# Layer 2 of a four-layer graph network: each node's own weights are formed and multiplied in four column tiles, after all supports

## The chip, the cores and the metric

The kernel runs on one core of one Trainium2 chip. The core has a matrix engine (TensorE, PE in the profile; its weight loads are listed apart as PEld), three elementwise engines (VectorE = DVE, ScalarE = ACT, GpSimd = POOL), a queue engine (SyncE = SP) and DMA queues. PE writes only to PSUM, a small memory of eight banks of 512 floats per partition; DVE and ACT carry results from PSUM to SBUF, the large on-chip memory. The metric is the device time of one execution in microseconds; lower is better. Before the change it is 1935.28 us, the median of 3 runs (1935.16 to 1940.87).

## The reference, cut to what matters

The input `x` is 8 x 2048 x 64 (batch B, nodes N, features), `adj` is a 2048 x 2048 matrix of zeros and ones. Four layers follow one another, each as `x = layernorm(x + layer(x, adj))`. The change is in layer 2 (a Chebyshev graph convolution with weights of its own for every node) and at the beginning of layer 3:

```python
def _L2_gnn_ref(x, node_embeddings, lap, weights_pool, bias_pool):   # lap = adj, CHEB_K = 3
    support_set = [jnp.eye(N, dtype=x.dtype), lap]
    for _ in range(2, CHEB_K):
        support_set.append(2.0 * lap @ support_set[-1] - support_set[-2])
    apt = jax.nn.softmax(jax.nn.relu(node_embeddings @ node_embeddings.T), axis=1)
    support_set.append(apt)
    supports = jnp.stack(support_set, axis=0)
    weights = jnp.einsum('nd,dkio->nkio', node_embeddings, weights_pool)
    bias = node_embeddings @ bias_pool
    x_g = jnp.einsum('knm,bmc->bknc', supports, x)
    x_g = jnp.transpose(x_g, (0, 2, 1, 3))
    out = jnp.einsum('bnki,nkio->bno', x_g, weights) + bias
    return out
```

`node_embeddings` is 2048 x 16 (d), `weights_pool` is 16 x 4 x 64 x 64 (d, k, i, o). So a node's output is a row of 4 x 64 = 256 support values times a 256 x 64 matrix, and that matrix is the sum of 16 pool matrices weighted by the node's embedding. Layer 3 takes three steps of `v = relu([v, adj v] W1 + b1) W2 + b2`.

## The kernel before, in words

**Data.** The batches go in pairs p = 0..3, so that 2 x 64 features fill the 128 partitions or the 128 columns of a tile. `adj` stays in SBUF for the whole kernel as 16 row tiles of 128 x 2048 in a form in which PE multiplies at one pass ("F32R"); the operand beside it is split into a high and a low part (`x_part[c]`, tags `v0h` to `v3l`), and both parts are multiplied. Nodes go in four chunks c of 512 columns, each with four tiles j of 128. A product with `adj` for one pair is 128 matmuls of 512 columns.

**PE order.** Every matmul and transpose goes through the helpers `mm` (L171) and `transpose` (L174), which pin PE to the order in which the program is written; `pin` does the same for a few operations of other engines. `later(n, f)` runs f after n further matmuls of the kind that call `tick`. PSUM has two pools here: `lps` with four one-bank buffers (tag `mm`) and `pph` with two two-bank buffers (tag `ph`).

**Layer 2.** The support `apt` is multiplied first (`ua`, plain float32). Then the function `supports()` is a generator: for each pair it yields the products `adj x` and `adj (adj x)`, one matmul at a time, and stores x, `adj x`, `adj adj x` and `apt x`, turned so that features are on partitions, into `xt_hbm`, `u1_hbm`, `u2_hbm`, `u3_hbm`. `fill(n)` takes n matmuls from it. The main loop of layer 2 (p, c, b, j, k) multiplies a tile of 128 nodes of one batch by the whole pool: the 256 support values are contracted in two matmuls (q = 0, 1), `wp[q][k]` holds 32 outputs x 16 embedding entries = 512 columns, and `py` receives, for each node and output, the 16 partial values. DVE then multiplies `py` by the node's 16 embedding entries (L1350) and adds the 16 up (L1351). After each such pair of matmuls `fill(2)` lets two matmuls of the supports through, as long as there are any.

```python
for q in range(2):
    mm(py, lhsT=a_z[q][:, cols(j, P)], rhs=wp[q][k], start=q == 0, stop=q == 1)
tick()
pr = fcav.rearrange("p i b f -> p (i b f)").rearrange("p (o d) -> p o d", d=D)
nc.vector.tensor_tensor(pr, py, e_b, ALU.mult)
nc.vector.tensor_reduce(r[:, j, b, cols(k, OH)], pr, AX.X, ALU.add)
fill(2)
```

At the end of a chunk the layer norm is taken (DVE L1362, ACT L148, DVE L150, POOL's power L154, DVE L155) and written back to `xn[p]`. The pool is centred beforehand (L1281 to L1289), so that the mean of the outputs is zero.

**Layer 3.** For p = 0, `first(c, n)` turns chunk c of `xn[0]` (`first_h`) and multiplies it by part of W1 (`factor`, which writes `x_part[c]`). The step loop accumulates `u` over all 16 tiles of `adj`, applies relu (L1506, L1508) and goes on. Between its tiles, `check()` compares a piece of `adj` with its rounded form.

Of the kernel before, what the change touches and what calls it, by code (L numbers as in the profile page):

```python
# [56 lines left out]
def tile_gnn_fast(  # L57
# [13 lines left out]
    w_pool: bass.AP,  # L71
# [152 lines left out]
    for i in range(12):  # L224
# [13 lines left out]
    xt_hbm, u1_hbm, u2_hbm, u3_hbm = (  # L238
        [dram.tile([P, N], F32, name=f"{name}_hbm{p}") for p in range(NP)] for name in ("xt", "u1", "u2", "u3")
    )  # L240
# [8 lines left out]
    adj = [adj_tile(adj_pool, t) for t in range(NT - XT)]  # L249
# [806 lines left out]
    xn += [xnp.tile([P, NT, P], F32, name=f"xn{p}") for p in range(NP)]  # L1056
# [141 lines left out]
    ready = set()  # L1198

# [7 lines left out]
    def turned_x(p, c):  # L1207
        pt = lps.tile([P, C], F32, tag="mm", name="pt", bufs=4)
        for j in range(JT):
            transpose(pt[:, cols(j, P)], xn[p][:, c * JT + j, :])  # L1210
        out_t(xt_hbm[p], c, pt, nc.scalar)

        bias = l2.tile([P, JT, 1, F], F32, tag="bias", name="bias", bufs=1)
        nc.sync.dma_start(bias[:, :, 0, :], bias_hbm[:, wide(c), :])
        x4 = xn[p][:, wide(c), :].rearrange("p t (b f) -> p t b f", f=F)
        nc.gpsimd.tensor_tensor(x4, x4, bias.to_broadcast([P, JT, 2, F]), ALU.add)

    def supports():

        for p in range(NP):  # L1220
            for k, hbm in ((1, u1_hbm), (2, u2_hbm)):
                chunks = [2, 3, 0, 1] if p == 0 and k == 1 else [*range(NCH)]
                uts = {}
                for g in range(2):
                    own = (2 * g, 2 * g + 1)
                    ug = pph.tile([P, 2, C], F32, tag="ph", name="u", bufs=2)
                    for q in chunks:
                        for t in range(q * JT, (q + 1) * JT):
                            for i in range(2):
                                for c in own:  # L1230
# [6 lines left out]
                                    yield  # L1237
                        if k == 1 and g == 0:
# [11 lines left out]
                    ready.add((p, k, g))  # L1250

    filler = supports()

    def until(*what):
        while what not in ready:
            fill(1)
# [7 lines left out]
    OD = F * D  # L1264
    OH = C // D
    emb_n = l2.tile([P, NT, D], F32, tag="e", name="emb_n")
    nc.gpsimd.dma_start(emb_n, emb.rearrange("(t p) d -> p t d", p=P))

# [7 lines left out]
    wp = [[l2.tile([P, OH, D], F32, tag=f"w{2 * q + k}", name=f"wp{q}{k}") for k in range(2)] for q in range(2)]  # L1276
    for q in range(2):
        for k in range(2):
            nc.gpsimd.dma_start(wp[q][k].rearrange("p o d -> p (o d)"), w_pool[q * P:(q + 1) * P, cols(k)])
    for k in range(2):  # L1280
        nc.vector.tensor_tensor(wp[0][k][0:F], wp[0][k][0:F], wp[1][k][0:F], ALU.subtract)  # L1281
        nc.vector.tensor_scalar(wp[1][k][0:F], wp[1][k][0:F], 2.0, None, op0=ALU.mult)
    sums = l2.tile([P, 2, 2, D], F32, tag="m", name="wp_m")
    for q in range(2):
        for k in range(2):
            nc.vector.tensor_reduce(sums[:, q, k, :], wp[q][k].rearrange("p o d -> p d o"), AX.X, ALU.add)
        nc.vector.tensor_tensor(sums[:, q, 0, :], sums[:, q, 0, :], sums[:, q, 1, :], ALU.add)
        for k in range(2):
            nc.vector.scalar_tensor_tensor(  # L1289
                wp[q][k], sums[:, q, 0:1, :].to_broadcast([P, OH, D]), -1.0 / F, wp[q][k],  # L1290
                op0=ALU.mult, op1=ALU.add,
            )

    halves = [slice(b * F, (b + 1) * F) for b in range(2)]
    lower, upper = halves
    xg = {}

    def load_xg(p, c, b):

        until(p, 2, c // 2)  # L1300
        a, z = (l2.tile([P, C], F32, tag=f"g{2 * b + q}", name=f"xg{b}{q}") for q in range(2))
        for dst, src in ((a[lower], xt_hbm), (a[upper], u1_hbm), (z[lower], u2_hbm), (z[upper], u3_hbm)):
            nc.sync.dma_start(dst, src[p][halves[b], cols(c)])
        xg[b] = a, z
# [29 lines left out]
    for b in range(2):  # L1334
        load_xg(0, 0, b)
    fill(20)
    for p in range(NP):
        for c in range(NCH):
            r = staged("r").rearrange("p t (b f) -> p t b f", f=F)
            for b in range(2):  # L1340
                a_z = xg[b]
                for j in range(JT):
                    e_b = emb_n[:, c * JT + j:c * JT + j + 1, :].to_broadcast([P, OH, D])
                    for k in range(2):
                        py = lps.tile([P, OH, D], F32, tag="mm", name="py", bufs=4)
                        for q in range(2):
                            mm(py, lhsT=a_z[q][:, cols(j, P)], rhs=wp[q][k], start=q == 0, stop=q == 1)
                        tick()
                        pr = fcav.rearrange("p i b f -> p (i b f)").rearrange("p (o d) -> p o d", d=D)
                        nc.vector.tensor_tensor(pr, py, e_b, ALU.mult)  # L1350
                        nc.vector.tensor_reduce(r[:, j, b, cols(k, OH)], pr, AX.X, ALU.add)  # L1351
                        fill(2)
                    if p == NP - 1 and c == NCH - 1 and b == 1 and j in (1, 2):

                        first(j - 1, 2)
                if c + 1 < NCH:
                    load_xg(p, c + 1, b)
                elif p + 1 < NP:
                    load_xg(p + 1, 0, b)
            r3 = r.rearrange("p t b f -> p t (b f)")  # L1360
            xs = xn[p][:, wide(c), :]
            nc.vector.tensor_tensor(r3, r3, xs, ALU.add)  # L1362
            layernorm(va, grouped(r3), grouped(xs), centred=True, small=l2, tag="x", bufs=2)

    STEPS = 3
    for c in (2, 3):  # L1370
# [892 lines left out]
```

## Time and profile before

| what | value |
|---|---|
| median of 3 runs | 1935.28 us (1935.16 to 1940.87) |
| span of the profiled execution (first to last instruction) | 1931.4 us |
| mean granted PE clock in it | 0.986 of full speed |
| busy in the span: PE / DVE / POOL / ACT | 1863.2 / 1010.8 / 533.5 / 393.9 us |
| layer 2's `apt` product | about 520 to 745 us |
| supports alone, then supports mixed with the pool product | 760 to 808 us, then 808 to about 1450 us |
| layer 3 | about 1450 us to the end |

The profiled execution has no time of its own beside its span; the median of the unprofiled runs lies 3.9 us above that span.

How to read it: the page gives busy time by engine, the chain of work that ended last, and groups of equal instructions. A row of a group reads: line, engine, operation, output <- inputs, shapes, count, then busy time and the mean duration of one in ns, then the idle time before it. A float32 matmul appears as two records. The duration of a PE record contains its way through the array, which overlaps with that of the next one; what a matmul costs in a stream is the distance from start to start.

### The profile page before, as it was taken

Reading aid. Unit: us, or ns where it says so; the run is one execution under the profiler, and the core shown is the slowest. Engines: PE = TensorE matmul, PEld = TensorE weight load, DVE = VectorE, ACT = ScalarE, POOL = GpSimd, SP = SyncE. Lnnn points to the kernel's source line nnn. Section 1 sums busy time; section 2 is a strip of 40 time slices with the busy share of each in tenths; the row PEclk is TensorE's granted clock in tenths of the full one; section 3 lists DMA queues with packets and bytes.
Section 4 is the critical chain, followed back from the end, with each engine's and each line's share of the span. In section 5 each row is a group of like instructions: output and inputs, shape, how many; then the busy total and the mean of one; then the engine's idle time right before and its main releaser. Section 6 shows DMA issues by size and latency. Waiting matters only on the chain.

```text
span 1931.4 us, 19557 instructions
## 1 busy us (share of the span) xinstructions
PE 1863.2 (96%) x7100; PEld 1211.2 (63%) x7100; DVE 1010.8 (52%) x1741; ACT 393.9 (20%) x771; POOL 533.5 (28%) x480
## 2 busy tenths in 40 slices
PE   6889899998999999999999999999999999999996
PEld 4667666666644445755755565565447878887875
DVE  6788756777422221466367636645784343333432
ACT  1446344343211111100100000010002222222211
POOL 3688645665344444111001101100001020100201
PEclk8999999999999999999999999999999999999998
DMA  9833343443300001211111110111101121121211
GB/s 321 292 92 115 124 150 123 158 143 118 98 0 28 28 22 45 93 44 52 45 36 52 56 45 22 60 56 36 44 22 41 44 60 44 50 54 45 57 26 24
DMA packets 94185, 143.10 MB, mean 74 GB/s; under 512 B 29232, under 2 KB 40112, under 8 KB 93696
## 3 DMA queue, kind: packets, MB, share of 16 engines
q1 hardware_dynamic: 83920, 105.39, 17.9%
q0 software_dynamic: 7760, 27.66, 4.4%
q10 hardware_dynamic: 2400, 8.72, 1.3%
q8 instruction: 58, 0.95, 0.2%
q14 instruction: 47, 0.39, 0.1%
HBM read 98.67 MB, written 43.06 MB: 73 GB/s over the span
## 4 chain that ended last, share of the span: by engine, by line
PE 83%; DMA 2%; DVE 1%; issue 1%; POOL 1%; ACT 1%; POOLq 0%; SPq 0%; ACTq 0%; DVEq 0%
PE u L171 37%; PE py L171 23%; PE ua L171 11%; PE ug L171 3%; PE pr L171 2%; PE pf L171 1%; PE po L171 1%; PE pt L174 1%; PE s L171 1%; PE pd L171 1%; PE pi L171 1%; DMA x<-x_hbm 0%; PE pn L174 0%; DMA xn<-in_emb 0%; PE pg L174 0%
## 5 line engine op out<-in xcount | busy, mean ns | idle before, releaser
L171 PE MATMUL py<-wp,xg 128*128 128x512 f32 x1024 | 475.2, 592 | 0.8 <-DMA xg<-u_hbm 0.8
L171 PEld LDWEIGHTS py<-wp,xg 128*128 128x128 f32 x1024 | 193.3, 189 | 161.5 <-issue 138.6
L1350 DVE TENSOR_TENSOR fcav<-py,emb_n 128x512 f32<-128x512 f32 x256 | 176.9, 691 | 135.1 <-PE py L171 129.3
L171 PE MATMUL ua<-pt,xn 128*128 128x512 f32 x512 | 230.2, 592 | 1.5 <-DVE pt L1131 1.5
L1351 DVE TENSOR_REDUCE r<-fcav 128x32 f32<-128x512 f32 x256 | 175.6, 686 | 8.2
L171 PEld LDWEIGHTS ua<-pt,xn 128*128 128x128 f32 x512 | 96.9, 190 | 111.2 <-issue 104.2
L154 POOL TENSOR_TENSOR ln_r<-ln_e,neg_half 128x8 f32<-128x8 f32 x32 | 53.5, 1671 | 399.2 <-DVE ln_e L152 369.8
L171 PE MATMUL u<-adj,v0h 128*128 128x512 f32 x384 | 148.0, 453 | 1.3 <-ACT h L1506 1.3
L171 PE MATMUL u<-adj,v2l 128*128 128x512 f32 x384 | 140.7, 431 | 1.3 <-DVE v2l L167 1.3
L171 PE MATMUL u<-adj,v2h 128*128 128x512 f32 x384 | 141.8, 436 | 0.0
L171 PE MATMUL u<-adj,v3l 128*128 128x512 f32 x384 | 140.1, 429 | 0.0
L171 PE MATMUL u<-adj,v3h 128*128 128x512 f32 x384 | 139.6, 430 | 0.0
L171 PE MATMUL u<-adj,v1h 128*128 128x512 f32 x384 | 139.3, 430 | 0.0
L171 PE MATMUL u<-adj,v0l 128*128 128x512 f32 x384 | 138.9, 429 | 0.0
L171 PE MATMUL u<-adj,v1l 128*128 128x512 f32 x384 | 137.9, 425 | 0.0
L1131 DVE TENSOR_SCALAR pt<-pt 128x512 f32<-128x512 f32 x64 | 30.3, 474 | 150.5 <-ACT pt L1130 150.3
L1137 POOL TENSOR_TENSOR acc<-acc,pt 128x512 f32<-128x512 f32 x60 | 76.4, 1274 | 107.1 <-DVE pt L1131 106.4
L1432 DVE SCALAR_TENSOR_TENSOR ar<-fcav,ar 128x512 f32<-128x512 f32 x64 | 45.7, 714 | 107.3 <-ACT ar L1431 107.3
L171 PEld LDWEIGHTS u<-adj,v0h 128*128 128x128 f32 x384 | 70.8, 189 | 37.4 <-issue 24.9
L171 PEld LDWEIGHTS u<-adj,v2l 128*128 128x128 f32 x384 | 72.9, 191 | 31.2 <-issue 14.9
L171 PEld LDWEIGHTS u<-adj,v3l 128*128 128x128 f32 x384 | 72.6, 190 | 30.2 <-issue 15.7
L171 PEld LDWEIGHTS u<-adj,v3h 128*128 128x128 f32 x384 | 72.8, 190 | 28.9 <-issue 14.3
(360 smaller groups left out, 2724.8 us busy)
## 6 DMA issues: line engine op xcount, KB each, us to landing
adj<-in_adj_t POOLq DMA_DIRECT2D x32, 512.0 KB, 6.9
fcav<-in_adj_t SPq DMA_DIRECT2D x64, 256.0 KB, 2.9
u_hbm<-ut SPq DMA_DIRECT2D x48, 256.0 KB, 2.4
xg<-u_hbm SPq DMA_DIRECT2D x96, 128.0 KB, 2.9
x_hbm<-r SPq DMA_DIRECT2D x28, 256.0 KB, 2.3
hs_hbm<-st ACTq DMA_DIRECT2D x8, 584.0 KB, 4.8
xt<-in_x_t SPq DMA_DIRECT2D x16, 256.0 KB, 6.0
ut<-u_hbm SPq DMA_DIRECT2D x16, 256.0 KB, 3.6
```

Of the source, the lines that this page charges most:

```text
L154: nc.gpsimd.tensor_tensor(rstd, vare, neg_half[:, :groups], ALU.pow)
L171: tc.keep_in_program_order(nc.tensor.matmul(*args, **kw))
L174: tc.keep_in_program_order(nc.tensor.transpose(dst, src, ident))
L1131: nc.vector.tensor_scalar(pt, pt, 1.0, None, op0=ALU.max)
L1137: nc.gpsimd.tensor_tensor(accs[c], accs[c], pt, ALU.add)
L1350: nc.vector.tensor_tensor(pr, py, e_b, ALU.mult)
L1351: nc.vector.tensor_reduce(r[:, j, b, cols(k, OH)], pr, AX.X, ALU.add)
L1432: nc.vector.scalar_tensor_tensor(ar.bitcast(F32), seen_a, 1.0, ar.bitcast(F32), op0=ALU.mult, op1=ALU.not_equal, accum_out=left[:, t, k:k ...
```

## The change

All supports now come first: the generator runs to its end before anything of the weights' product starts. Its gaps on the other engines take in, as a list `aside`, the preparation of the pool and of the embeddings.

Then come 16 units u = (c, k): eight node chunks c of 256 nodes, and two halves k of the contraction (x and `adj x`; `adj adj x` and `apt x`). Each unit has two parts.

- `produce` forms the weights of its 256 nodes: for each output o a matmul of 64 rows (16 embedding entries in four combinations of high and low parts) x 128 columns (two supports x 64 inputs), 256 nodes wide, in F32R. Two of them, for two outputs, lie in the lower and the upper half of PE's rows. ACT and DVE carry the PSUM results into `w_all` (128 partitions x 256 nodes x 64 outputs), three copies in five on ACT. A copy takes 2 outputs x 256 nodes and writes them node by node, 64 floats apart.
- `consume` multiplies four nodes at a time: the stationary operand is 32 columns (8 batches x 4 nodes), the moving operand the four nodes' weights, 256 columns, plain float32. Four such matmuls, for four groups of nodes, lie in the four column tiles of PE. Of the 4 x 4 node pairs that come out only the diagonal is wanted; DVE selects and adds it with the 0/1 columns `own4`.

At a chunk's end (`chunk_end`) the sums go to HBM and come back with nodes on partitions, and the layer norm follows in six steps (store, load, add, square, power, scale) at fixed places of the next two units; the result goes to `x3_hbm`. Since `w_all` and `sums_2` need room, nine of the 16 tiles of `adj` are lent and loaded again from HBM after the last unit. The first step of layer 3 for p = 0 is written out as `opening`, which multiplies with the tiles that stayed while the others load.

```diff
-    adj = [adj_tile(adj_pool, t) for t in range(NT - XT)]
+    LEND, LENT = 6, 8
...
+    def lent_tiles():
+
+        one = adj_pool.tile([P, N], F32R, tag="one", name="adj_one")
+        more = adj_pool.tile([P, LENT, N], F32R, tag="more", name="adj_more")
+        return [column_halves(one)] + [column_halves(more[:, k, :]) for k in range(LENT)]
+
+    adj = [adj_tile(adj_pool, t) for t in range(LEND)] + lent_tiles()
...
+                            if aside and (p, k) >= (1, 1) and t % 2:
+                                if aside[0][0] <= (p, k):
+                                    aside.pop(0)[1]()
...
-    for b in range(2):
-        load_xg(0, 0, b)
-    fill(20)
-    for p in range(NP):
-        for c in range(NCH):
-            r = staged("r").rearrange("p t (b f) -> p t b f", f=F)
-            for b in range(2):
-                a_z = xg[b]
-                for j in range(JT):
...
-                        for q in range(2):
-                            mm(py, lhsT=a_z[q][:, cols(j, P)], rhs=wp[q][k], start=q == 0, stop=q == 1)
-                        tick()
...
-                        nc.vector.tensor_tensor(pr, py, e_b, ALU.mult)
-                        nc.vector.tensor_reduce(r[:, j, b, cols(k, OH)], pr, AX.X, ALU.add)
-                        fill(2)
...
+    for _ in filler:
+        pass
+    second_stack()
+    w_all = adj_pool.tile([P, Q, F], F32, tag="more", name="w_all")
+    w_four = w_all.rearrange("p (m n) o -> p n m o", m=4)
+    sums_2 = adj_pool.tile([P, 2, O4, F], F32, tag="one", name="sums_2")
+    count = [0]
+
+    def produce(u, between):
+
+        c, k = divmod(u, 2)
+        for s in range(O4):
+            if s % 4 < 2:
+                banks = [lps.tile([P, 2, Q], F32, tag="mm", name="pw", bufs=4) for _ in range(2)]
+            else:
+                both = pph.tile([P, 2, C], F32, tag="ph", name="pw", bufs=2)
+                banks = [both[:, i, :].rearrange("p (o n) -> p o n", o=2) for i in range(2)]
+            for i in range(2):
+                q, o = divmod(2 * s + i, 4)
+                for j, r in enumerate(halves):
+                    mm(banks[j][:, i, :], lhsT=wst[k][q][r, o, :], rhs=est[c][r, :], start=True, stop=True)
+            for j in range(2):
+                dst = w_all[:, :, 4 * s + 2 * j:4 * s + 2 * j + 2].rearrange("p n o -> p o n")
+                count[0] += 1
+                if 3 * count[0] % 5 < 3:
+                    pin(nc.scalar.copy(dst, banks[j]))
+                else:
+                    pin(nc.vector.tensor_copy(dst, banks[j]))
+            if s in between:
+                between[s]()
+
+    def consume(u, between):
+
+        c, k = divmod(u, 2)
+        total = sums_2[:, c % 2]
+        x8 = xg.pop(u)
+        for v in range(O4 // 4):
+            py = pph.tile([P, 4, 4, F], F32, tag="ph", name="py", bufs=2)
+            for i in range(4):
+                for j in range(4):
+                    n = O4 * j + 4 * v + i
+                    mm(py[32 * j:32 * (j + 1), i], lhsT=x8[:, n], rhs=w_four[:, n], start=True, stop=True)
+            dst = total[:, 4 * v:4 * v + 4, :]
+            for m in range(4):
+                if m == 0 and k == 0:
+                    pin(nc.vector.tensor_scalar(dst, py[:, :, m, :], own4[:, m:m + 1], None, op0=ALU.mult))
+                else:
+                    pin(nc.vector.scalar_tensor_tensor(
+                        dst, py[:, :, m, :], own4[:, m:m + 1], dst, op0=ALU.mult, op1=ALU.add
+                    ))
...
+            if k == 0:
+                store()
+                in_p = {6: load, 12: add, 14: square}
+                in_c = {1: power}
+            else:
+                in_p = {2: scale}
...
+        produce(u, in_p)
+        consume(u, in_c)
+        if k == 1:
+            waiting = chunk_end(c)
+    adj[LEND:LEND + 1 + LENT] = lent_tiles()
+    for t in [*range(LEND + 1, LEND + 1 + LENT), LEND]:
+        for g in range(2):
+            load_adj(t, g)
...
+    def opening():
...
+        for c in range(2):
+            own_term(c)
+        work = passes([*range(LEND)])
...
+        while waiting:
+            waiting.pop(0)()
+        for q in range(1, NP):
+            xn[q] = xnp.tile([P, NT, P], F32, tag=f"xn{q - 1}", name=f"x3{q}")
+            nc.sync.dma_start(xn[q], x3_hbm[q])
+        for _ in passes([*range(LEND + 1, 12), LEND]):
+            pass
+        first_turn(3)
+        factor(3, h[3], bd_e, None)
+        own_term(3)
+        later(1, lambda: [with_bias(0, c) for c in range(NCH)])
+        for n, _ in enumerate(passes([*range(12, NT)])):
...
```

`passes(tiles)` multiplies chunks 0 and 1, then 2 and 3, with the tiles it is given: four matmuls a tile and half. `second_stack` loads the pool's second half into the buffers of `x_part`.

## The prediction

> **What bounds the kernel now.** I read the page's busy times and clock first, then the chain of work that ended last, then the groups.
>
> ```profile
> span 1931.4 us, 19557 instructions
> ...
> PE 1863.2 (96%) x7100; PEld 1211.2 (63%) x7100; DVE 1010.8 (52%) x1741; ACT 393.9 (20%) x771; POOL 533.5 (28%) x480
> ...
> PE u L171 37%; PE py L171 23%; PE ua L171 11%; PE ug L171 3%; PE pr L171 2%; PE pf L171 1%; PE po L171 1%; PE pt L174 1%; PE s L171 1%; PE pd L171 1%; PE pi L171 1%; DMA x<-x_hbm 0%; PE pn L174 0%; DMA xn<-in_emb 0%; PE pg L174 0%
> ...
> L171 PE MATMUL py<-wp,xg 128*128 128x512 f32 x1024 | 475.2, 592 | 0.8 <-DMA xg<-u_hbm 0.8
> ...
> L1350 DVE TENSOR_TENSOR fcav<-py,emb_n 128x512 f32<-128x512 f32 x256 | 176.9, 691 | 135.1 <-PE py L171 129.3
> ```
>
> PE is the bound, and `py`, the matmuls that the change removes, is 23% of the chain; its DVE companion waits for PE, so it is cover, not path. The busy time of each engine in layer 2's two stretches (columns as in the page, then clock, DMA share, GB/s) says the same:
>
> ```profile
> 760.00:808.00 48.00, 48.00 (x223) 38.90 (x222) 16.00 (x24) 6.98 (x12) 14.16 (x14) 1.00 0.39 133
> 808.00:1455.00 647.00, 646.22 (x1973) 361.04 (x1972) 405.31 (x607) 41.46 (x70) 55.05 (x39) 1.00 0.13 43
> ```
>
> Start to start, the chain has 144 `py` records in 61.80 us, 0.429 each, and 16 `u` records in 3.73, 0.233 each. So `py` costs 1024 x 0.429 = 439.5 us, and the supports 8 products x 128 x 0.233 = 239 whether mixed or alone.
>
> **What the Trainium skill says.** (1) "TensorE: Matmul & The Clock Gate", "Part 3: Packing small matmuls — row/col tiling": matmuls in different row or column tiles run concurrently; three column tiles gave 2.38 times, four row tiles 3.07. This trace agrees for two. Its timeline of PE, in layer 0, with start, length and count:
>
> ```profile
> 240.61 1.13 PE L171 MATMUL pf<-ind,fcav 64*128 64x512 f32 x4
> 241.58 1.02 PE L171 MATMUL pf<-gt,fcav 64*128 64x512 f32 x4
> ...
> 454.37 1.08 PE L171 MATMUL pd<-t,fcav 128*64 128x512 f32 x4
> 455.38 0.73 PE L171 MATMUL u<-adj,v2h 128*128 128x512 f32 x2
> ```
>
> `pf` is two matmuls in two row tiles, `pd` two in two column tiles; each pair has four records. They take 0.97 and 1.01 us to the next start, where four records in turn would take 1.72 and perfect overlap 0.86. (2) "TensorEngine Tiling (Array Packing)", "PSUM Bottleneck": tiling speeds up TensorE but not the way out of PSUM. This is my main point below. (3) "Vector Engine (DVE) Microarchitecture Reference", "5.2 Measured stream behaviour on trn2 (trn3 not measured)": a port streams at full rate only in runs of two adjacent words; an output that hops at every element took 1.71 ns a column against 1.05, one stepping 24 words 2.5. The trace has the like on the reading side: the reduction of `wp` that reads 16 words apart took 1019 ns, a contiguous one of its size (L1351) 686. Strided writing of 512 elements, by ACT above all, is in no row.
>
> ```profile
> L1286 DVE TENSOR_REDUCE wp_m<-wp x4: 1015/1019/1031, 774.5 to 778.3; 128x16 f32<-128x512 f32 x4
> ```
>
> (4) the first page, "HAM oscillation — how this bites in real kernels": a PE idle for some 3.4 us falls to half clock. The windows agree (the number before the last two is the clock):
>
> ```profile
> 476.00:480.00 4.00, 1.03 (x5) 0.51 (x3) 2.36 (x7) 1.17 (x2) 2.90 (x3) 0.96 0.91 312
> 480.00:484.00 4.00, 2.06 (x9) 1.98 (x10) 2.75 (x6) 1.30 (x4) 1.59 (x2) 0.50 0.97 367
> ```
>
> **Removed:** 439.5 us on the path. The 352 us of L1350 and L1351 were hidden.
>
> **Added: the eviction in `produce`.** A unit has 32 copies of 128x512, 19.2 on ACT and 12.8 on DVE. PE makes their input with 64 F32R matmuls of 256 columns: at half of 0.233 each 7.5 us in turn, about 4 in pairs; either is under the copies. Back to back, ACT needs 0.48 us a copy from start to start (the timeline of ACT):
>
> ```profile
> 1447.58 0.59 ACT L166 CAST v0h<-pr 128x512 fp32r<-128x512 f32 x1 [3.74 <-PE pr L171]
> 1448.06 0.59 ACT L1311 COPY h<-pt 128x512 f32<-128x512 f32 x1
> ```
>
> DVE's contiguous ones stand 0.61 apart (L167, 1465.15 and 1465.76). But these copies write one word at every 64. From below, the step is free: ACT 19.2 x 0.48 = 9.2, DVE 12.8 x 0.61 = 7.8. By page (3), 1.71 ns instead of ACT's 0.83: 0.48 + 512 x 0.88 = 0.93, so ACT 17.9 us; DVE by the trace's 333 ns more, 0.94, so 12.0. At 2.5 ns ACT has 1.33, 25.6 us. I take 0.93, as 64 words is a long hop; that ACT pays as DVE does is an assumption. DVE also begins some 1.7 us late (below), 13.7, so ACT sets the end.
>
> **Added: `consume`.** No copy of the next unit may write `w_all` before the last matmul of this one has read it, and no matmul may start before the last copy: the two parts are in series. 64 matmuls of 256 columns in 16 groups of four tiles. One costs 2 records x 0.214 = 0.43; four in perfect overlap 0.43, so 6.9 us; with the overhead that `pd` shows (1.01 - 0.86 = 0.15) 0.58, so 9.3, which I take; all in turn 27.5. The 32-column loads have no row; I leave them hidden as those of `pd` are. DVE's 16 selections of 128x256 are like L606 (416 ns): 1.7 us behind each four groups (2.3 us), hidden but for the last four, which delay DVE's first copies. PSUM's eight banks let ACT go on.
>
> **Between them:** the passage through the array (a record lasts 0.40 with 0.233 between starts) twice, and the first pair of the next unit: 0.7. The layer norm: two squares on ACT every second unit, 0.5 a unit. Its chain (store and load near 3 us each, two POOL additions at 1.3, after DVE's last selection and SP's issues of 0.34) reaches the squares some 13 us into a unit; they stand after 15/16 of 17.9, so nothing waits. With free writes it would: 2 us a unit. POOL's steps and the reductions on DVE lie in slack.
>
> Unit: 9.3 + 0.7 + 17.9 + 0.5 = 28.4 us, 16 of them 454 us.
>
> **Moved: the supports** lose their mixture but were at 48.00 of 48.00 us of PE without it. The pool's preparation, some 40 to 50 us of DVE in 60 us, lies beside them (DVE was busy 16 of 48 there); without that cover, 10 us. The loads of 2 MB by `second_stack` lie under the first unit. Start of the first unit: 2 us.
>
> **Added: the loan of `adj`.** 18 transfers of 0.5 MB follow the last matmul of the last unit on POOL's queue (18 x 0.55 us of issue), which nothing urgent shares.
>
> ```profile
> adj<-in_adj_t POOLq DMA_DIRECT2D x32, 512.0 KB, 6.9
> ```
>
> 9.4 MB at the 400 GB/s that the windows of layer 0 show are 24 us, 7 to the first landing, and 3 MB of `xn` on SP's queue compete: tile 6, loaded last, lands after about 33. PE has until then the own terms and turns (5), 48 matmuls (11) and five tiles of the first half (5): 12 us idle, and half clock afterwards, 3: 15, between 5 and 30. SP's chain for the last chunk (15 us) ends earlier.
>
> **Sum:** 1931.4 - 439.5 + 454 + 2 + 15 = 1963 for the span; the median of the runs lay 3.9 above it, so **1967 us**. Break-even is a unit of (439.5 - 17) / 16 = 26.4, an ACT copy of 0.83.
>
> **Rivals.**
> - *Strided writes cost ACT little.* Place: the copies to `w_all`. Speaking for it: the page's rows are DVE's alone, writes could be buffered. At 0.48 ACT ends after 9.2 and DVE sets the end: 13.7 if it pays (unit 24.2, 1900 us), 9.5 if not (unit 22.2 with the squares' wait, 1868). If ACT pays by half, 1915. It decides below 0.83 us. Chance 0.27.
> - *Something in the unit is dearer.* The step costs 2.5 ns: unit 36.1, 2091 us. PE, with bursts of 0.3 us every 1.2 in `produce`, falls to half clock and needs 2 us more a unit: 1999; against it, windows with 2.3 to 3 of 4 us busy keep full clock. Four column tiles run in turn: 2258; `pd` speaks against it. Together 0.20.
> - *Transfers are the bound*: 2 x 1 MB of operands and 256-byte rows of `y_hbm` per two units. The trace stores 128 KB in such rows in 2.1 us; I give it 0.03 (near 2030).
>
> **How the numbers follow.** My forecast has 0.50; its own range is 1930 to 2000 (consume 7 to 11 us, copy 0.88 to 0.97). The range 1880 to 2060 leaves out some 0.08 below (both engines free) and 0.11 above. A difference of 0.3%, 6 us, is about what a measurement can tell. Faster: 0.26 of the first rival and 0.05 of the forecast; same: 0.05 and 0.01; slower: the rest, 0.63.
>
> **What would show it.** In the profile after: `py` at L171 gone from the chain; ACT COPY `w_all` x307 near 0.93 us start to start and DVE near 0.94 (right), or 0.6 (wrong, the first rival); groups of four `py` matmuls 0.58 apart; ACT over 60% busy in the units; a gap of about 12 us at PE before tile 6 in `opening`, released by DMA `adj`; no clock below 0.9 in the units. The prediction falls most easily with the ACT copy, since 0.1 us there is 31 us of the sum.

## The result, and the profile after

The changed kernel takes 2021.85 us (median of 4 runs, 2017.73 to 2026.2) against 1936.03 of the kernel before on the same chip: ratio 1.0438, 95% interval 1.0417 to 1.0459. It is slower, as forecast, but by 4.4% and not by 1.6%: 2022 us lies in the range of 1880 to 2060 and outside the forecast's own of 1930 to 2000. The page of the changed kernel, its head and its chain:

```profile
span 2015.9 us, 24123 instructions
...
PE 1750.4 (87%) x9148; PEld 1219.0 (60%) x9148; DVE 982.8 (49%) x1703; ACT 679.2 (34%) x1086; POOL 576.7 (29%) x522
...
PEclk9999999998999999999976766766768999999998
...
PE u L172 23%; ACT w_all L1459 6%; PE py L172 6%; DVE w_all L1461 4%; DVE sums L1481 3%; PE pr L172 2%; PE pw L172 1%; DMA y_hbm<-sums 1%; PE po L172 1%; DVE sums L1479 0%; DVE ln_v L1521 0%; ACT xb L1516 0%; DMA y<-y_hbm 0%; PE pt L175 0%; DMA raw<-in_w 0%
```

PE was busy for 96% of the span and is for 87% of a longer one. `py` fell from 23% of the chain to 6%, and in its place stand ACT's and DVE's copies (`w_all`) and DVE's selections (`sums`); the row of the granted clock has a valley where the units are. The groups concerned (busy time, mean ns of one, then the idle time before them):

```profile
L1459 ACT COPY w_all<-pw 128x512 f32<-128x512 f32 x307 | 279.2, 1074 | 193.4 <-PE pw L172 174.6
...
L1461 DVE COPY w_all<-pw 128x512 f32<-128x512 f32 x205 | 191.5, 1047 | 70.2 <-ACT w_all L1459 67.7
L172 PE MATMUL py<-w_all,xg 128*32 128x256 f32 x2048 | 157.5, 470 | 68.2 <-ACT w_all L1459 35.2
...
L1481 DVE SCALAR_TENSOR_TENSOR sums<-py,marks,sums 128x256 f32<-128x256 f32 x224 | 107.5, 483 | 44.0 <-PE py L172 37.1
```

A record's duration overlaps with the next one's, so what a copy costs is busy time by count: ACT 279.2 / 307 = 0.909 us, DVE 191.5 / 205 = 0.934. The forecast had 0.93 and 0.94. The dearest term of the sum was right, and the excess must be elsewhere. The three stretches by engine (columns as in the prediction): the supports, the 16 units, the beginning of layer 3.

```profile
745.00:1027.00 282.00, 266.24 (x1168) 211.36 (x1167) 70.65 (x89) 45.50 (x70) 50.41 (x35) 0.98 0.41 119
1027.00:1521.00 494.00, 329.18 (x3103) 204.88 (x3102) 325.30 (x500) 287.57 (x326) 57.97 (x46) 0.67 0.29 64
1521.00:1600.00 79.00, 64.08 (x288) 49.73 (x287) 19.41 (x40) 11.03 (x18) 14.65 (x21) 0.91 0.60 193
```

In the units no engine is busy all the time: PE 329 of 494 us, DVE 325, ACT 288 (58%, a little under the 60% that the prediction gave as a sign). In the supports PE, which had been busy in 48.00 of 48.00 us, is idle for 15.8. Cut at the first support product, at the first and the last matmul of the weights' product and at the end, the two profiled spans give this account in us. (The supports of before, mixed with the pool product, are taken from the run with all supports first, below. Of its layer 2, 754.5 to 1451.25, 696.8 - 439.5 - 254.9 = 2.4 us are layer 3's; they are put into the last row.)

| stretch | before | after | difference | forecast |
|---|---|---|---|---|
| up to the first product of the supports | 754.5 | 751.1 | -3.3 | 0 |
| supports | 254.9 | 276.6 | +21.7 | +2 |
| weights' product | 439.5 | 491.6 | +52.1 | +14.5 |
| layer 3 and what follows | 482.5 | 496.5 | +14.0 | +15 |
| span | 1931.4 | 2015.9 | +84.5 | +31.5 |

The first row scatters from one execution to the next (751.1 to 758.8 in the runs below), so it says nothing. Of 53 us too many, 37.6 are in the units (30.7 us each instead of 28.4) and 19.7 in the supports; the first and the last row give 4.3 back, and the last came as forecast.

**The unit.** The timeline of the changed kernel with start, length, what and how often, and in brackets the idle time before it and what ended it; then windows over the beginning of this unit's forming, over the rest of it, and over the first node matmuls (the number before the last two is the granted clock):

```profile
1197.08 7.87 PE L172 MATMUL py<-w_all,xg 128*32 128x256 f32 x96 [3.49 <-ACT w_all L1459]
...
1205.47 1.96 PE L172 MATMUL py<-w_all,xg 128*32 128x256 f32 x32 [0.52 <-DVE sums L1481]
...
1238.22 3.66 ACT L1459 COPY w_all<-pw 128x512 f32<-128x512 f32 x4 [11.24 <-PE pw L172]
...
1241.06 4.51 DVE L1461 COPY w_all<-pw 128x512 f32<-128x512 f32 x5
...
1243.93 2.77 ACT L1459 COPY w_all<-pw 128x512 f32<-128x512 f32 x3 [2.05 <-DVE w_all L1461]
```

```profile
1177.00:1181.00 4.00, 1.64 (x22) 1.29 (x20) 3.82 (x8) 2.79 (x3) 4.00 (x4) 1.00 0.38 111
1182.00:1194.00 12.00, 8.18 (x43) 5.65 (x43) 9.73 (x12) 10.69 (x13) 0.00 (x0) 0.50 0.55 111
...
1197.00:1201.00 4.00, 3.92 (x40) 1.80 (x44) 0.20 (x1) 0.03 (x1) 0.00 (x0) 0.50 0.00 0
1201.00:1205.00 4.00, 3.95 (x64) 2.19 (x56) 3.35 (x8) 0.00 (x0) 0.00 (x0) 0.86 0.00 0
```

Three things are to be seen. First the clock: the node matmuls begin after a pause of 3.49 us, since PE is eight banks ahead of the copies and has nothing left to do, but the clock fell long before it. In each of the first 15 units it goes to half 3.7 to 5.5 us after the first `pw`, in the forming, where PE works in short pieces between the copies, and before any pause of more than 2.1 us; it stays at half through the pause and some 5 us into the node matmuls. Then the pace: the last 32 records, two for each matmul, are four groups of four: 1.96 / 4 = 0.49 us a group, cheaper than the 0.58 of the forecast, but they waited 0.52 us for DVE: there are two buffers for `py`, and 16 selections with 0.52 us from start to start (a record lasts 0.483) take 8.3 us. And after the selections, ACT makes four copies and then stands for 2.05 us, because the next buffer's contents wait for DVE, which has only just come from its last selection (1241.06). Over all units ACT waits so 29 times:

```profile
ACT w_all L1459 <- DVE w_all L1461: 18.8, 29, 2.1
```

**The supports.** The waits of PE between 745 and 1027 us (sum, times, longest), and the timeline around one:

```profile
PE pn L175 <- DVE ut L1210: 8.6, 2, 5.8
PE u L172 <- DVE v3l L168: 4.0, 1, 4.0
PE u L172 <- ACT v0h L167: 2.4, 1, 2.4
```

```profile
802.37 3.58 DVE L1336 TENSOR_REDUCE sums<-raw 128x64 f32<-128x2048 f32 x1 [4.64 <-DMA raw<-in_w]
...
806.61 1.22 PE L172 MATMUL u<-adj_more,v3l 128*128 128x512 f32 x2 [4.03 <-DVE v3l L168]
```

With a fourth line of 0.7 us these are 15.7 us. DVE's low part `v3l`, for which PE waits, stood behind a reduction of the pool of 3.58 us that had begun just before. The two matmuls after it take 1.22 us instead of 0.63: half clock again. The waits are 15.7 of the 21.7 us; the other 6 are about what a clock of 0.98 instead of 1.00 costs in 282 us (5.6, an estimate from the window above).

**Layer 3.** The timeline of the queues and of the wait at the end of the reload:

```profile
1521.53 2.24 SPq L1494 DMA_DIRECT2D y_hbm<-sums  x4
...
1548.29 2.67 SPq L1506 DMA_DIRECT2D y<-y_hbm  x4
1548.70 1.06 POOL L211 DMA_DIRECT2D adj_one<-in_adj_t  x2 [11.60 <-DMA y_hbm<-sums]
...
1553.68 1.22 PE L172 MATMUL u<-adj_one,v1h 128*128 128x512 f32 x2 [13.08 <-DMA adj_one<-in_adj_t]
```

The gap before tile 6 is 13.08 us, near the 12 of the forecast, but not for its reason. `adj_one` lies where the sums lay, so it may be loaded only after the last sums are stored; that store is issued from 1521.5 on, 1.6 us after the first of the reloads, and lands only at 1548, though the stores of the earlier chunks' sums took about 3 us. That it stands behind the reloads at the DMA engines is likely (they are busy for 92% of the time between 1520 and 1550), but no run separates it.

### The profile page after: what moved, and what is told of

It is laid out like the page before. It is cut to its first block, busy times and chain, and to the rows that moved or that the text cites. A ratio compares the mean times of both kernels' runs of the same rounds, so it can differ in the third digit from the quotient of the medians.

```text
span 2015.9 us, 24123 instructions
## 1 busy us (share of the span) xinstructions
PE 1750.4 (87%) x9148; PEld 1219.0 (60%) x9148; DVE 982.8 (49%) x1703; ACT 679.2 (34%) x1086; POOL 576.7 (29%) x522
## 4 chain that ended last, share of the span: by engine, by line
PE 33%; DVE 9%; ACT 7%; issue 3%; DMA 2%; POOL 0%; SPq 0%; ACTq 0%; POOLq 0%; DVEq 0%
PE u L172 23%; ACT w_all L1459 6%; PE py L172 6%; DVE w_all L1461 4%; DVE sums L1481 3%; PE pr L172 2%; PE pw L172 1%; DMA y_hbm<-sums 1%; PE po L172 1%; DVE sums L1479 0%; DVE ln_v L1521 0%; ACT xb L1516 0%; DMA y<-y_hbm 0%; PE pt L175 0%; DMA raw<-in_w 0%
## 5 line engine op out<-in xcount | busy, mean ns | idle before, releaser
L1459 ACT COPY w_all<-pw 128x512 f32<-128x512 f32 x307 | 279.2, 1074 | 193.4 <-PE pw L172 174.6
L172 PE MATMUL pw<-est,wst 64*128 64x256 f32 x1024 | 165.8, 423 | 96.3 <-ACT w_all L1459 33.1
L1461 DVE COPY w_all<-pw 128x512 f32<-128x512 f32 x205 | 191.5, 1047 | 70.2 <-ACT w_all L1459 67.7
L172 PE MATMUL py<-w_all,xg 128*32 128x256 f32 x2048 | 157.5, 470 | 68.2 <-ACT w_all L1459 35.2
L172 PEld LDWEIGHTS pw<-est,wst 64*128 64x128 f32 x1024 | 114.8, 264 | 148.7 <-ACT w_all L1459 64.5
L1481 DVE SCALAR_TENSOR_TENSOR sums<-py,marks,sums 128x256 f32<-128x256 f32 x224 | 107.5, 483 | 44.0 <-PE py L172 37.1
L172 PE MATMUL u<-adj_more,v2h 128*128 128x512 f32 x384 | 125.5, 405 | 0.0
L172 PE MATMUL u<-adj_more,v2l 128*128 128x512 f32 x384 | 123.9, 399 | 0.0
L172 PE MATMUL u<-adj_more,v3l 128*128 128x512 f32 x288 | 95.3, 407 | 4.0 <-DVE v3l L168 4.0
L172 PE MATMUL u<-adj_more,v3h 128*128 128x512 f32 x288 | 93.7, 404 | 0.0
```

Source lines behind the costliest of these rows:

```text
L172: tc.keep_in_program_order(nc.tensor.matmul(*args, **kw))
L1459: pin(nc.scalar.copy(dst, banks[j]))
L1461: pin(nc.vector.tensor_copy(dst, banks[j]))
L1481: pin(nc.vector.scalar_tensor_tensor(dst, py[:, :, m, :], own4[:, m:m + 1], dst, op0=ALU.mult, op1=ALU.add))
```

## The experiments

Each ratio is to runs of the kernel before on the same chip; their medians were 1935.42, 1934.03, 1935.74 and 1935.19 us. A unit's length is the distance from the first `pw` to the last `py`, divided by 16.

**1. Contiguous copies.**

```diff
-dst = w_all[:, :, 4 * s + 2 * j:4 * s + 2 * j + 2].rearrange("p n o -> p o n")
+dst = w_all.rearrange("p n o -> p (n o)")[:, cols(2 * s + j)].rearrange("p (o n) -> p o n", o=2)
```

> The copies into w_all write 512 adjacent floats instead of one float at every 64; everything else stays, so the weights lie in another order than the matmuls of consume read them and the output is not the reference's. Theory (the one-word step of the write makes the copies long, and ACT's copies set the length of a unit): ACT from 0.91 to about 0.49 us a copy, DVE from 0.94 to about 0.62; the copies of a unit then last about 10 to 11 us instead of 19, 16 units save 125 to 145 us: about 1885 us. Rival (the copies are long because two engines read PSUM while PE writes it, or because of the hand-over of banks): copies stay near 0.9 us and the time near 2020 us.

Measured: 1917.83 us, ratio 0.9912 (0.9884 to 0.994). The row of the copies on ACT (min / median / max of one in ns):

```profile
L1459 ACT COPY w_all<-pw x307: 565/605/766, 1029.6 to 1409.4; 128x512 f32<-128x512 f32 x154
```

The output is not the reference's, as the expectation says, and the weights' new order lets some node matmuls begin before the last copies, so that run 2 is the cleaner measure of the whole. But the copies' own time is clear: the step of 64 words in the write is what makes them long. The time falls by 104 us and the units shrink from 30.7 to 24.5. The first rival, that the step costs ACT little, falls. The expected 1885 us are not reached, and the trace says why: ACT now waits 28.3 us in all for buffers that DVE holds and 12.3 us for POOL's sums ahead of the squares, which the prediction had named for the case of free writes. That these waits set the limit is read from the trace, not tested.

**2. Copies in pairs of outputs, the hop on the reading side.** They go node by node and write two adjacent words; PSUM is read with a hop of 256 words.

```diff
-dst = w_all[:, :, 4 * s + 2 * j:4 * s + 2 * j + 2].rearrange("p n o -> p o n")
+dst = w_all[:, :, 4 * s + 2 * j:4 * s + 2 * j + 2]
...
-pin(nc.scalar.copy(dst, banks[j]))
+pin(nc.scalar.copy(dst, banks[j].rearrange("p o n -> p n o")))
...
-pin(nc.vector.tensor_copy(dst, banks[j]))
+pin(nc.vector.tensor_copy(dst, banks[j].rearrange("p o n -> p n o")))
```

> The copies keep their place in w_all but go node by node: two adjacent outputs are written as a pair, and the hop moves to the reading side, where the two outputs lie 256 floats apart in a PSUM bank. Theory A (only SBUF makes a hop dear): ACT near 0.5 us a copy, about 1885 us, and this would be a usable version. Theory B (a hop costs the same on the PSUM side): copies stay at 0.9 to 1.0 us and the time at 2020 us or a little above.

Measured: 1924.54 us, ratio 0.9941 (0.992 to 0.9962).

```profile
L1459 ACT COPY w_all<-pw x307: 567/617/849, 1032.8 to 1416.0; 128x512 f32<-128x512 f32 x154
```

617 ns against 605, on DVE 682 against 681: the hop in PSUM costs next to nothing, and so does the step of 64 words in SBUF as long as two words are written at each. The copies keep their place, so this is the price of the single words: 97 us of the whole, 30.7 to 24.7 in a unit. This one edit turns the change from 4.4% slower into 0.6% faster (interval 0.4 to 0.8%), with the same result; the 1885 us of theory A are missed by 40, for the reason given under run 1.

**3. Each matmul of the forming three times over**, to keep PE at full clock.

```diff
+for _ in range(3):
     for i in range(2):
         q, o = divmod(2 * s + i, 4)
         for j, r in enumerate(halves):
             mm(banks[j][:, i, :], lhsT=wst[k][q][r, o, :], rhs=est[c][r, :], start=True, stop=True)
```

> Every matmul of produce is issued three times into the same place (same result), 2048 matmuls more in all, so that PE stays busy while the copies run. Theory (PE falls to half clock in produce, and the first groups of consume pay for it about 2 us in each of 16 units): the clock in the units rises from 0.67 to above 0.9, consume falls from about 10.3 to about 8.3 us, and the kernel gets faster by 25 to 35 us: about 1990 us. Rival (the clock costs nothing because the copies set a unit's length, or the further 10 us of PE work per unit delay the copies): 2022 us or above.

Measured: 2023.41 us, ratio 1.0458 (1.043 to 1.0486); the mean clock rose from 0.902 to 0.959.

```profile
1205.58 7.46 PE L172 MATMUL py<-w_all,xg 128*32 128x256 f32 x96 [3.34 <-ACT w_all L1460]
```

No gain. The clock is now full to the end of the forming and falls only after the pause ahead of the node matmuls, which stays (3.34 us here), since it is the time that the copies need for the last banks. The node matmuls get 0.5 us shorter (9.9 instead of 10.4, mean of the units), and the rest of a unit 0.6 longer, above all because the first bank is full only after the third pass: ACT's first copy begins 1.0 us after the last node matmul instead of 0.5. So the run shows no net gain; it doesn't show that the clock costs nothing.

**4. The kernel before, with all supports first.** One part of the change alone.

```diff
+for _ in filler:
+    pass
 for b in range(2):
     load_xg(0, 0, b)
-fill(20)
```

> The kernel before with one edit: all supports run before the pool product instead of being mixed with it. Theory (PE is full in both orders, so the order alone costs nothing): 1936 us within 6 us. Rival (the mixture hid waits of the supports or DVE's work on py, and a part of what the change lost is the order itself): 1946 us or more.

Measured: 1933.16 us, ratio 0.9986 (0.9975 to 0.9998): at most 0.3% shorter.

```profile
745.00:1010.00 265.00, 264.18 (x1179) 209.59 (x1178) 37.26 (x56) 36.99 (x65) 48.70 (x40) 1.00 0.19 67
```

PE is busy in 264.18 of 265 us. The order costs nothing; what slows the supports is what the change put beside them.

**5. Three times the matmuls, and only the four one-bank buffers for the forming**, so that PE gets less far ahead.

```diff
-if s % 4 < 2:
-    banks = [lps.tile([P, 2, Q], F32, tag="mm", name="pw", bufs=4) for _ in range(2)]
-else:
-    both = pph.tile([P, 2, C], F32, tag="ph", name="pw", bufs=2)
-    banks = [both[:, i, :].rearrange("p (o n) -> p o n", o=2) for i in range(2)]
+banks = [lps.tile([P, 2, Q], F32, tag="mm", name="pw", bufs=4) for _ in range(2)]
+for _ in range(3):
...
```

> Three times the matmuls of produce, as in the run warm3, and produce takes only the four one-bank buffers, so that PE is at most four copies ahead of ACT and DVE and its pause before consume gets shorter than the 3.3 us seen in warm3. Theory (the half clock at the beginning of consume costs some 1.7 us in each unit): the first 32 records of py take about 2.0 us instead of 3.3 to 3.7, and the kernel is 20 to 30 us faster than the changed one: about 1995 us. Rival (consume is limited by DVE's selections, not by PE, so the clock costs little; or four buffers hold the copies up): 2015 us or above.

Measured: 2058.09 us, ratio 1.0643 (1.0622 to 1.0664), units of 32.8 us.

```profile
1217.79 3.69 PE L172 MATMUL py<-w_all,xg 128*32 128x256 f32 x64 [1.77 <-ACT w_all L1456]
```

In this unit the pause is down to 1.77 us, and the first 64 records take 3.69 us: full clock from the first on, and node matmuls of 8.1 us. It is so in 9 of the first 15 units, with pauses of 1.4 to 2.3 us; in the other six, with pauses of 2.0 to 3.1, the clock still falls. The mean of the node matmuls is 9.0 us in place of 10.4. But the copies, with half the buffers, lost more.

**6. Four buffers alone**, without the threefold matmuls.

> The changed kernel with the weights formed only in the four one-bank buffers; the two two-bank buffers serve the selections alone. One part of the run with threefold matmuls in four banks done alone. Theory (four buffers hold up the copies by 3 to 4 us a unit, but the engines come to the unit's end with less in front of PE, so that PE's pause before the node matmuls falls below 2 us and the first 32 records run at full clock, which is worth 2 us a unit): units of 31.5 to 33 us, 2035 to 2060 us. If the threefold matmuls were what held that run up: within 8 us of 2022, or below it where the shorter pause is worth more than the missing buffers (down to 1995).

Measured: 2059.66 us, ratio 1.0647 (1.0631 to 1.0663), units of 33.0 us. So the missing buffers cost 2.3 us a unit. Here too the pause is short, 1.87 us, yet the first 64 records took 5.12 us: a short pause doesn't suffice if the clock has fallen in the forming, as it does here in every unit. Against this run the threefold matmuls of run 5 shorten the node matmuls by 1.2 us (10.2 to 9.0) and lengthen the rest of a unit by 1.0, so that 0.2 us a unit remain.

**7. The pool not centred.** What this leaves out is named in the expectation.

```diff
-        lambda: centre_raw(2),
-        lambda: centre_raw(0),
...
-        lambda: centre_raw(1),
...
-        lambda: centre_raw(3),
```

> The centring of the pool is left out (the four reductions of 3.6 us and the four subtractions of 2.3 us on DVE during the supports); the mean of layer 2's output is then not removed and the output is not the reference's. Theory (these long DVE instructions stand ahead of the splits and copies on which the supports' matmuls wait, and cost most of the 16 us that PE idles between 745 and 1027 us): PE idles under 5 us there, and the kernel is 10 to 14 us faster: about 2009 us. Rival (the supports' waits come from running alone, without the mixture): no gain, 2020 us.

Measured: 2004.97 us, ratio 1.0362 (1.0342 to 1.0383), 17 us less. The waits of PE between 745 and 1030 us:

```profile
PE u L172 <- ACT v0h L167: 3.2, 1, 3.2
...
PE u L172 <- DVE v0l L168: 0.7, 1, 0.7
```

The supports last 259.7 us instead of 276.6, which is the whole gain. The waits for `ut` and `v3l`, 12.6 of the 15.7 us, are gone; the 3.9 us that remain are those of the first split. With run 4 this settles the greater part of the supports: PE waits for small copies and splits that stand behind the centring of the pool on DVE.

**8. The pool's reductions and subtractions cut into four.**

```diff
-nc.vector.tensor_reduce(s, raw[k].rearrange("p o i -> p i o"), AX.X, ALU.add)
+for i in range(4):
+    nc.vector.tensor_reduce(s[:, cols(i, 16)], raw[k][:, :, cols(i, 16)].rearrange("p o i -> p i o"), AX.X, ALU.add)
```

> The changed kernel with the pool's reductions and centrings on DVE each cut into four shorter instructions; the work is the same. Theory (the 15.7 us by which PE waits in the supports are queueing behind DVE instructions of 2.3 to 3.7 us, and turned supports come later than one such instruction because of its length): an instruction of about 1 us fits into the time that PE has in hand, so PE's waits between 745 and 1027 us fall from 15.7 to 4 to 6 us and the time to 2008 to 2012 us. Rival (DVE's work as a sum is too much for the stretch, or the planner puts the four parts one behind the other): the waits stay near 15 and the time stays within 5 us of 2022.

Measured: 2015.81 us, ratio 1.0412 (1.0395 to 1.0429), 6 us less; PE's waits fell to 11.6 us, not to 4 to 6. The timeline of DVE ahead of the longest of them:

```profile
858.55 3.99 DVE L1337 TENSOR_REDUCE sums<-raw 128x16 f32<-128x512 f32 x4 [5.82 <-DMA raw<-in_w]
...
863.32 2.50 DVE L1345 SCALAR_TENSOR_TENSOR raw<-sums,raw 128x512 f32<-128x512 f32 x4
865.86 2.29 DVE L1351 TENSOR_TENSOR raw<-raw 128x2048 f32<-128x2048 f32 x1
868.06 0.68 DVE L1210 COPY ut<-u 128x512 f32<-128x512 f32 x1
```

Elsewhere `ut` slipped in between two parts (at 933.95 and 952.05 us), but here all parts stand one behind the other, and after them an instruction that stayed whole (`combine`, 2.29 us), ahead of the copy `ut` that PE waits for: 6.3 us. That the pool's work delays PE is shown by run 7; that its length in one piece does is shown, at most, for the third that this run gained. (In run 9, which edits nothing here, the supports were 4.0 us shorter too, and the wait for `v3l` 1.7 us instead of 4.0, so that a part of the 6 us may be a change of order alone.) The order in which DVE gets this work I didn't change on its own.

**9. ACT takes the first four copies of a unit and then every second one** (18 to 14 instead of 19.2 to 12.8).

```diff
-if 3 * count[0] % 5 < 3:
+if s < 2 or j == 0:
```

> ACT takes the first four copies of each unit and then every second one (18 on ACT, 14 on DVE, instead of 19.2 and 12.8), so that DVE, which is still selecting the last sums, is not on the way of the first buffers. Theory (ACT's copies set the length of produce, and ACT waits up to 2 us for buffers that DVE holds): 1.2 copies at 0.91 us less and 0.6 us less waiting in each unit, 25 to 30 us: about 1993 us. Rival (DVE with its selections is as long as ACT): within 8 us of 2021 us.

Measured: 1981.42 us, ratio 1.0246 (1.0218 to 1.0275), 40 us less, more than expected.

```profile
1196.59 15.00 ACT L1459 COPY w_all<-pw 128x512 f32<-128x512 f32 x17 [11.90 <-PE pw L172]
```

ACT runs through 17 copies without a stop. The units take 28.3 us. Two terms make up about the 2.4 us gained on each: 1.2 copies less on ACT, 1.1 us, and ACT's waits for buffers that DVE holds, 18.8 us in all in the changed kernel, 1.2 a unit, and none here. The run changes both together; the share of each is the trace's, not an experiment's.

**10. Tile 6 loaded after tile 11** instead of last.

```diff
-for t in [*range(LEND + 1, LEND + 1 + LENT), LEND]:
+for t in [*range(LEND + 1, 12), LEND, *range(12, LEND + 1 + LENT)]:
```

> After the last unit the lent tile 6 is loaded after tile 11 instead of last, so that the POOL queue waits for the store of the last sums before it starts the last three tiles. Theory (the store of the last sums, issued at 1521 us, lands only at about 1548 us because the transfers of eight tiles stand ahead of it at the DMA engines; tile 6 and the last layer norm wait for it): the pause of 13 us before tile 6 shrinks to some 3 us and the kernel is 8 to 12 us faster: about 2011 us. Rival (the pause is the transfer time of the 9.4 MB, as the prediction had it): no gain.

Measured: 2023.62 us, ratio 1.0465 (1.0442 to 1.0488): no gain.

```profile
1549.21 1.22 PE L172 MATMUL u<-adj_one,v1h 128*128 128x512 f32 x2 [5.33 <-DMA adj_one<-in_adj_t]
...
1565.58 0.48 PE L175 MATMUL pt<-ident,x 128*128 128x128 f32 x1 [7.39 <-DVE x L1530]
```

The gap fell from 13.08 to 5.33 us, and PE came to the turn of the last chunk's layer norm before that was ready, and waited 7.39 us there. Both waits hang on the store of the last sums, which lands only at 1544 here too.

**11. Four edits together:** the pairs of run 2, the share of run 9, the cuts of run 8, and both squares moved behind the first four selections:

```diff
-                in_p = {6: load, 12: add, 14: square}
-                in_c = {1: power}
+                in_p = {6: load, 12: add}
+                in_c = {0: square, 1: power}
```

> The changed kernel with four edits together: copies that write two outputs side by side and hop in PSUM, ACT taking the first four copies of a unit and then every second one (18 to 14), both squares moved behind the first four selections of the node matmuls, and the pool's long DVE instructions cut into four. Theory (the terms of the sum are separate: copies and hand-over on one side, supports on the other): from the 1925 us of the pair-wise copies, 30 to 45 us less for the hand-over (copies now cost 0.52 instead of 0.91 us, so that less of the wait for buffers lies on the path than the 40 us found with slow copies), 10 for the supports, 8 to 10 for the squares' wait: 1860 to 1880 us, 3% under the kernel before. Rival (with copies this short PE or DVE sets the unit, PE at half clock through all of the forming, so that the hand-over no longer counts): the time stays between 1895 and 1915.

Measured: 1881.68 us, ratio 0.973 (0.9716 to 0.9743), units of 22.2 us. It is 2 us above the expectation. The terms very nearly add: the 97, 40 and 6 us of runs 2, 9 and 8 would give 1878. What moving the squares is worth was not measured alone.

**12. The same, and each matmul of the forming twice.**

> The kernel with the four edits together (1881.7 us), and each matmul that forms the weights issued twice; the result is the same, PE has 64 matmuls more in a unit. Here PE has a pause of only 1.6 us before the node matmuls, and the mean clock between 1027 and 1400 us was 0.77. Theory (what is left of the clock's price is that PE is too little occupied while it forms weights, so that the first 32 records of a unit's node matmuls take 3.5 us instead of 1.9): doubled, the forming keeps PE at full clock and stays under DVE's copies, so each unit loses 1.5 to 2 us: 1850 to 1860 us, clock above 0.9 there. Rival (doubled matmuls at half clock are longer than the copies, 16 us against 11): units longer by 2 to 4 us, 1910 to 1945 us.

Measured: 1864.54 us, ratio 0.9636 (0.962 to 0.9652), the fastest of all. A window over most of the units:

```profile
1027.00:1400.00 373.00, 312.46 (x4214) 243.84 (x4210) 272.74 (x525) 172.09 (x309) 65.94 (x60) 0.94 0.46 108
```

The clock there is 0.94 (0.77 in run 11), and doubling PE's work in the forming saved 17 us, about 1.1 us a unit instead of the 1.5 to 2 expected. The profile is that of the slowest of the four executions (1872.26 us), and its units, 21.7 us, are shorter by only 0.5: the node matmuls by 1.1 (9.9 to 8.8), while the rest got 0.6 longer. In 5 of its first 15 units the first 64 records still took 5.3 us and not 3.69, after a pause that was about 1.66 us in all of them.

## Why the prediction was right in direction and wrong in size

Two steps failed that the sum had put at nothing: the cover for DVE's late start in the units (19 us), and the supports without their mixture (19.7 us). A third, the node matmuls, was too small by 18 us, as half clock and the pace of DVE had been left out. A unit in us:

| term | forecast | measured |
|---|---|---|
| `consume`, the node matmuls | 9.3 | 10.4 |
| ACT's 19.2 copies | 17.9 | 17.5 |
| ACT's waits for buffers that DVE holds | 0 | 1.2 |
| passages and squares | 1.2 | 1.6 (the remainder) |
| sum | 28.4 | 30.7 |

- **Removed, 439.5 us: right.** `py` of the old kind is gone, and the order of the supports by itself costs nothing (run 4). The supports alone take 254.9 us and not 239, since the transposes between the products (11 us) were not counted; this doesn't enter the sum.
- **The copy, 0.93 us on ACT and 0.94 on DVE: right** (0.909 and 0.934), and so is its reason. The prediction's assumption, that ACT pays for a hop in the write as the Trainium skill's "Vector Engine (DVE) Microarchitecture Reference", "5.2 Measured stream behaviour on trn2 (trn3 not measured)", states it for DVE, holds for writes to SBUF: without the hop 605 ns for one copy's record on ACT, with it 1074. It doesn't hold for hops on the side of PSUM (run 2), which the forecast didn't use. The prediction also quoted that runs of two adjacent words keep the full rate, and didn't ask whether the copies could be written so; run 2 does just that.
- **"PSUM's eight banks let ACT go on": this step failed.** The statement is about buffers, but their order is fixed: three copies in five are ACT's, the others DVE's. PE can't form what comes next until DVE, still at the last unit's selections, has emptied its own. The cover for DVE's late start was ACT's work, and ACT ran dry, in the unit shown after four copies: 18.8 us of waits in all. Run 9 removes them, together with 1.2 copies a unit, and puts the unit at 28.3 us, by chance almost the 28.4 that the sum had.
- **`consume`, 9.3 us: it took 10.4, after two errors of opposite sign.** At full clock it takes 8.1 us (runs 5 and 12): the group of four is 0.49 us and not 0.58, but selections follow each other at 0.52 us, while the forecast took L606's 0.416, so that DVE, with two buffers ahead, sets the pace. "Hidden but for the last four" was wrong. Half clock at the beginning adds 2.3.
- **"No clock below 0.9 in the units": wrong**, the mean is 0.67. I had asked whether bursts in the forming keep the clock up, found windows of the kernel before that spoke for it, and given the rival 2 us a unit. The bursts don't keep it up, and the 2.3 us that it costs in the node matmuls is the rival's size. Each run that brought the clock back paid for it in the forming, so that of 0.5 to 1.2 us gained in the node matmuls between nothing (run 3) and 0.5 us (run 12; by its median 1.1) was left.
- **The preparation of the pool, "without that cover, 10 us": this step failed.** The sum had nothing for it. I had summed DVE's work (40 to 50 us in a stretch in which it is idle for two thirds) and found room. Not the sum but the place counts: 15.7 us of PE's waits and 6.0 more in the same stretch, with half clock after the waits: 19.7 above the forecast's 2. Runs 4 and 7 show it from both sides.
- **The loan of `adj`, 15 us: right in size (14) by luck, wrong in cause.** "SP's chain for the last chunk ends earlier" was wrong: its store lands at 1548, and the tile loaded last is waiting for it.
- **The rivals.** Free writes for ACT (0.27) are out by run 1: without the step the change is a gain of 0.9%. Transfers as the bound: no, the DMA engines are busy for 29% of the units. "Something in the unit is dearer" (0.20) is what came, beside the supports. Of its three mechanisms the half clock came, and the price of 2.5 ns a word and the column tiles in turn did not; ACT's waits for DVE were not among them.

What stays open: how the supports' waits split between the length of DVE's instructions and their order; why the last store lands so late; and what full clock would be worth in a unit if it cost nothing in the forming.

## What to carry to other kernels

When two engines empty one row of buffers in a fixed order, the one that comes late stops both: give the first buffers after a change of work to the engine that is free. When work is moved beside a bound engine, don't compare sums of busy time, but ask how long each small step that the bound engine waits for can stand behind a long one. And where a copy out of PSUM must hop, try the hop on the side that is read, with two adjacent words written at each place: here that made a copy as short as a contiguous one.

## What was not expected of the hardware

- A copy of 512 elements a partition on ACT has a record of 1074 ns where it writes single words 64 apart to SBUF (0.909 us by count), and of 617 ns with two adjacent words at each hop, nearly as good as contiguous (605); the hop of 256 words in PSUM costs next to nothing. DVE: 1047 (0.934 us by count), 682 and 681 ns.
- Four column tiles of plain float32, 32 columns each and 256 wide, take 0.49 us for the four, at full clock, against 0.43 for one of them in a stream of its own by the prediction's count.
- In the forming of the changed kernel the clock fell to half within 3.7 to 5.5 us in each of the first 15 units, though PE had no pause of more than 2.1 us until then; with three times the matmuls it stayed full until the next pause (run 3, all units but the last).
- After a pause of 2.7 to 4.8 us the clock fell even where it had been full until then (run 3). After 1.66 us it stayed full in 10 of 15 units of run 12, after 1.4 to 2.3 us in 9 of 15 of run 5; after 1.4 to 3.1 us in none of run 6, where it had fallen before the pause.
- Twice the matmuls in the forming, for the same result, made a kernel faster by 0.9% (run 12 against run 11).
